# When the scans' last columns are copied out: one step later from SBUF, behind the product with C from PSUM

## The chip, the cores and the metric

The program runs on one core of one Trainium2 chip. The metric is the device time of one execution in microseconds (us). The kernel before was timed in three runs: 12873.15, 12877.57 and 12906.72 us, median 12877.57 us. One further execution was recorded by the hardware profiler; it took 12896.13 us and its span, first to last instruction, is 12894.0 us. All lines of the profile below are of that one execution.

The engines are called as in the profile: PE (TensorE, matrix products; PEld is its loading of weights), DVE (VectorE), ACT (ScalarE), POOL (GpSimd) and SP (SyncE, which here issues most of the DMA transfers). An engine works through its own instructions in the order in which they stand in its queue; an instruction that has to wait for another engine holds up all that stand behind it.

## The reference

Eight images of 64 channels and 64 x 64 pixels pass through four layers, all in float32. Layer 0 is full attention over the 4096 pixels of an image, followed by convolutions. Layer 1 is two blocks of window attention with an MLP each. Layer 2 is a dynamic 3 x 3 filter and a 1 x 9 convolution. Layer 3 is a selective scan in four directions, with norms, a gate and a convolutional mixer. The change lies in layer 3's scan:

```
def step(h, inp):                       # once per pixel, 4096 times, for each image and direction
    u_t, dt_t, B_t, C_t = inp           # u, dt: 128 channels; B, C: 16 states
    h = h * exp(dt_t[..., None] * A) + dt_t[..., None] * B_t[:, :, None, :] * u_t[..., None]
    return h, einsum('bkcn,bkn->bkc', h, C_t)
```

So each of 128 x 16 states follows its own first-order recurrence over 4096 pixels, and the output of a pixel is the sum over the 16 states of h times C.

## The kernel before

**Tiling.** The images are worked in four pairs, p = 0 to 3. An image has four directions of 4096 pixels, cut into 8 chunks of 512 (`TD`). One chunk of one direction of one image is a *unit*; a pair has 64 units. A unit's 128 channels x 16 states are taken in 8 *steps*; a step has two scans, j = 0 and j = 1, of 128 partitions x 512 pixels each (one partition is one channel with one state; two states of 64 channels lie in a tile). So a pair has 512 steps, and the whole kernel 2048 steps and 4096 scans.

**A step** (`step`, L1769 to L1807). For each j, ACT computes exp(dt * A) into a PSUM bank `dad` (L1789). DVE then scans: it takes `dad` as the factor, the tile `vd` (dt * B * u) as the addend and, unless the chunk is its row's first, the column of `carries` that was kept from the chunk before (L1792). The scan's result goes to one of two places. `own` says how many of a step's two scans DVE carries through alone: such a scan is written back into its own PSUM bank (`dad<-dad`), and DVE multiplies it with C itself (L1806 on DVE). The other scans are written to an SBUF tile `hd`, and POOL multiplies them with C, one at a time (L1806 on POOL) or both at once (L1803). `own` is 0 and 1 in turn in the first three pairs, 1 and 2 while layer 0's attention runs beside the scans (`dense`), and 1, 1, 1, 2 in the last pair.

**The copies.** The last column of each scan (the first one, where the direction runs backward) is what the next chunk's scan of the same state starts from, 8 steps later. ACT copies it into `carries`: for a scan in PSUM one column, for a scan in SBUF one column, or both columns of a step in one instruction where both scans lie in SBUF (L1794 to L1800). There are 3008 such copies. In the program they stand directly behind their scan, so j = 0's copy stands ahead of j = 1's exp, and j = 1's copy ahead of DVE's product with C. The PSUM bank is kept apart between engines: of two instructions on different engines that read one bank, the later in the program waits for the earlier. So DVE's product with C (L1806) waits for ACT's copy (L1800) of the same `dad`.

**Beside it.** POOL computes `vd` = B * (dt * u) for both scans of a step (`products`, L1767) two steps ahead. B and C of a step are two rows each, spread over 64 partitions by DMA from memory (`fetch`, L1759; SP's queue), four buffers each. PE sums the products over the states into the unit's bank `yd` (`sums`, L1818), and DVE adds it to the image's result `Y` (`gather`, L1831 to L1836). For the following unit, SP loads `xs` (`load`, L1722), PE, ACT and DVE work out dt and dt * u (`inputs` and `spread`, L1730 to L1748), and SP spreads them over the partitions into `du` (L1752), from which both the exps and POOL's products read. The exps' banks, tag `da`, are three; `inputs` takes its banks from the same three.

**The order of the work.** `scans` (L1672) goes through the 512 steps of a pair and puts pieces of other work between them: layers 0 to 2 and layer 3's preparation of the next pair (`front`) and the rest of layer 3 of the pair before (`back`), at a rate by estimated costs, so that they end 24 steps (`LEAD`) before the pair does. The first pair's front runs alone, ahead of all scans, together with layer 0 of the second. The last pair has only `back` beside it, of the pair before and then its own. This program order is not yet the engines' order: when the program is built, a scheduler places each engine's instructions by it, but lets an instruction pass others that are not yet ready by the scheduler's own estimate. In the built program many exps stand ahead of copies that precede them in the source.

Of the kernel before, what the change touches and what calls it, by code (L numbers as in the profile page):

```python
# [10 lines left out]
AF = mybir.ActivationFunctionType  # L11
# [13 lines left out]
TD = 512  # L25
NTD = L // TD
# [212 lines left out]
class _Net:  # L239
    def __init__(self, ctx, tc, x, packs, layout, out):  # L240
        self.tc, self.nc = tc, tc.nc
        self.x, self.out = x, out
        nc = self.nc
        self.const = ctx.enter_context(tc.tile_pool(name="const", bufs=1))
        self.dram = ctx.enter_context(tc.tile_pool(name="rows", bufs=2, space=bass.MemoryType.DRAM))
        self.packs, self.layout, self.w = packs, layout, {}
        self.load(self.const, (0, 1))
        with tc.tile_pool(name="temp", bufs=1) as temp:
            self.load(temp, (2,))
            self.prepare()  # L250
# [910 lines left out]
class _Direct:  # L1161
# [8 lines left out]
    def __init__(self, net, ctx):  # L1170
        self.net, self.tc, self.nc, self.w = net, net.tc, net.nc, net.w
        tc = self.tc
        self.dram = ctx.enter_context(tc.tile_pool(name="mem", bufs=2, space=bass.MemoryType.DRAM))
        self.slabs = ctx.enter_context(tc.tile_pool(name="slabs", bufs=3))
        self.ps = ctx.enter_context(tc.tile_pool(name="ps_scan", bufs=3, space=PSUM))
        self.pf = ctx.enter_context(tc.tile_pool(name="ps_front", bufs=3, space=PSUM))
        self.kept = {}
        self.turn = -1
        self.dense = 0

    def begin(self, ctx):


        tc = self.tc
        with tc.tile_pool(name="slabs0", bufs=3) as slabs, tc.tile_pool(name="w00", bufs=2) as pool:
            ahead = _Apart(self, slabs, pool).first(1)
            front = first = done = 0
            for cost in self.front(0):
                front += cost
                if cost == 0:  # L1190
                    first = front
                while first and done < AHEAD * (front - first):
                    done += next(ahead, front)
            self.run(ahead)
        one = ctx.enter_context(tc.tile_pool(name="scan1", bufs=1))
        self.Y = one.tile([P, L], F32, name="Y", tag="Y")
        self.carries = one.tile([P, NST], F32, name="carry", tag="carry")
        self.sw = ctx.enter_context(tc.tile_pool(name="scan", bufs=2))
        return front, first
# [472 lines left out]
    def scans(self, p, beside, cost):  # L1672

        self.units = []
        for im in range(2):
            out = self.memory("ys")
            self.kept["y", 2 * p + im] = out
            for nth, k in enumerate((1, 3, 0, 2)):  # L1680
                order = range(NTD) if k < 2 else range(NTD - 1, -1, -1)
                self.units += [dict(image=2 * p + im, k=k, c=c, at=at, nth=nth, out=out) for at, c in enumerate(order)]
        self.load(self.units[0])
        self.inputs(self.units[0])
        self.spread(self.units[0])
        n = 8 * len(self.units)

        late = self.back(p) if p == B // 2 - 1 else None
        steps = [{} for _ in range(n)]
        done = 0  # L1690
        for i in range(-3, n):
            if i + 3 < n:
                self.fetch(i + 3, steps[i + 3], 0)
            if 0 <= i + 2 < n:
                self.fetch(i + 2, steps[i + 2], 1)
                self.products(i + 2, steps[i + 2])
            if i >= 0:
                self.step(i, steps[i])
                for j in self.DUE[i % 8]:
                    if i + j >= 0:  # L1700
                        self.sums(i + j, steps[i + j], steps[i]["w"])
                if i % 8 == 2 and i > 8:
                    self.gather(self.units[i // 8 - 1])
                if p == B // 2 - 1 and done >= cost:
                    self.turn = max(self.turn, 0)
                while done < cost * (i + 1) / (n - LEAD):
                    done += next(beside, cost)
            if late and i >= n - 8 * (NTD - 1) and i % 8 in (3, 5, 7):
                next(late)
            if i >= 0 and i % 8 < 3 and i // 8 + 1 < len(self.units):  # L1710
                (self.load, self.inputs, self.spread)[i % 8](self.units[i // 8 + 1])
        for i in (n - 2, n - 1):
            self.sums(i, steps[i])
        self.gather(self.units[-1])
        self.run(beside)
        if late:
            self.run(late)
# [51 lines left out]
    def step(self, i, st):  # L1769

        nc, w, net = self.nc, self.w, self.net
        wk, ps = self.sw, self.ps
        u = self.units[i // 8]
        k, c, at, CC, v = u["k"], u["c"], u["at"], st["C"], st["v"]


        n0 = 2 * (i % 8)
        own = 1 + (i % 4 == 3) if u["image"] >= B - 2 else i % 2 + self.dense
        rev = k >= 2

        def along(t):
            return t[:, ::-1] if rev else t

        h = wk.tile([P, 2 - i % 2, TD], F32, name="hd", tag=f"h{i % 2}", bufs=2)
        hs = []
        for j in range(2):
            n = n0 + j
            da = self.bank("dad", (P, TD), "da")
            nc.scalar.activation(da, u["du"][:, j, 0], AF.Exp, scale=net.As[:, k, n : n + 1])  # L1789
            first = 0.0 if at == 0 else self.carries[:, n : n + 1]  # L1790
            to = da if j >= 2 - own else h[:, j]
            nc.vector.tensor_tensor_scan(along(to), along(da), along(v[:, j]), first, ALU.mult, ALU.add)  # L1792
            hs.append(to)
            if at < NTD - 1 and (own or j):  # L1794
                ends = h[:, :, 0] if rev else h[:, :, TD - 1]
                cs = self.carries[:, n0 : n0 + 2]
                if own:
                    ends = to[:, 0:1] if rev else to[:, TD - 1 : TD]
                    cs = self.carries[:, n : n + 1]
                nc.scalar.activation(cs, ends, AF.Copy)  # L1800

        if own == 0:
            st["w"] = nc.gpsimd.tensor_tensor(v, h, self.twice(CC), ALU.mult)  # L1803
        for j in range(2 if own else 0):
            engine = nc.vector if j >= 2 - own else nc.gpsimd
            m = engine.tensor_tensor(v[:, j], hs[j], CC, ALU.mult)  # L1806
            st.setdefault("w", m)  # L1807

    def sums(self, i, st, after=None):

        nc, w, net = self.nc, self.w, self.net
        wk, ps = self.sw, self.ps
        u = self.units[i // 8]
        k, c = u["k"], u["c"]
        if i % 8 == 0:
            u["y"] = ps.tile([P, TD], F32, name="yd", tag="y", bufs=1)
        for j in range(2):
            m = nc.tensor.matmul(  # L1818
                u["y"][self.HALF[j]], lhsT=w["fold"], rhs=st["v"][:, j], start=(i % 8 == 0), stop=(i % 8 == 7)
            )  # L1820
            if after is not None and j == 0:
                net.behind(m, after)
# [169 lines left out]
```

## Time and profile before

| | |
|---|---|
| median of three runs | 12877.57 us |
| profiled execution: its own time, its span | 12896.13 us, 12894.0 us |
| granted TensorE clock over the span | 0.817 of full speed |
| front of pair 0 (and layer 0 of pair 1), no scans | 0 to 2196 us |
| scans of pair 0, beside them layers 1 and 2 and layer 3's preparation of pair 1 | 2196 to 4516 us |
| scans of pair 1: beside `back` of pair 0 | 4516 to 4950 us |
| ... beside layer 0's attention of pair 2 | 4950 to 5680 us |
| ... beside the rest of pair 2's front | 5700 to 7500 us |
| scans of pair 2, in the same three parts | 7583 to 10643 us |
| scans of pair 3: with `back` of pair 2, 24 of 64 units | 10643 to about 11400 us |
| ... alone, and then with `back` of pair 3 | about 11400 to 12780 us |
| the rest of `back` of pair 3 | to 12894 us |
| ACT's copies (L1800) | 3008; 168 ns each from PSUM, 201 ns from SBUF |
| exp (L1789), scan (L1792), product with C on DVE (L1806) | 681, 1270 and 677 ns each |

A unit of 8 steps takes about 36 us in pair 0 and 33 us in pair 3. Times of waits in the profile are idle time of an engine, put down to the instruction that ended it; idle time of an engine that is not the bottleneck costs nothing by itself.

### The profile page before, as it was taken

To read this page: it belongs to the slowest core of one execution; us is meant where nothing else is said; L and a number is where in the kernel's file an instruction comes from. 1 tells how busy PE (TensorE), PEld (TensorE's weight loads), DVE (VectorE), ACT (ScalarE), POOL (GpSimd) and SP (SyncE) were. 2 spreads that over 40 slices of the span, in tenths; PEclk is the share of its full clock that TensorE was granted. 3 is DMA by queue.
4 is the path that set the end of the run, shared out by engine and by line. 5 is a ranking of instruction groups with operands and counts; after the bars stand their busy time and mean duration, and the time that the engine had idled before them with its cause. 6 is when DMAs were issued, how large, how long until landed. Compare 5 with 4: busy or idle time off the path is not lost. (4 is left out here: it accounts for less than half of the span.)

```text
span 12894.0 us, 141975 instructions
## 1 busy us (share of the span) xinstructions
PE 9714.9 (75%) x46358; PEld 3162.6 (25%) x46358; DVE 8570.4 (66%) x10061; ACT 7066.2 (55%) x15577; POOL 7760.9 (60%) x3875
## 2 busy tenths in 40 slices
PE   9999985788786558988888556997898655555556
PEld 2243421333221112224332111222342101111111
DVE  0121245788878785467776778358776778998888
ACT  5556523565646655655654645665654645455444
POOL 0000001999899883457765795347775698877774
PEclk9999976787787678988888667998888767777667
DMA  0000002555555552334443564234443456556553
GB/s 25 1 1 1 1 13 87 160 165 158 159 162 167 177 162 84 98 119 128 139 124 108 168 182 129 70 104 135 136 123 105 142 179 192 172 167 187 173 172 125
DMA packets 779985, 1579.99 MB, mean 123 GB/s; under 512 B 89312, under 2 KB 89440, under 8 KB 778208
## 3 DMA queue, kind: packets, MB, share of 16 engines
q1 hardware_dynamic: 755040, 1514.49, 38.5%
q10 hardware_dynamic: 24192, 56.32, 1.1%
q8 instruction: 367, 6.01, 0.2%
q14 instruction: 386, 3.16, 0.1%
HBM read 1199.26 MB, written 102.76 MB: 101 GB/s over the span
## 5 line engine op out<-in xcount | busy, mean ns | idle before, releaser
L1767 POOL TENSOR_TENSOR vd<-B,du 128x1024 f32<-128x1024 f32 x2048 | 4816.6, 2370 | 3728.7 <-DMA B<-rows 2391.2
L1818 PE MATMUL yd<-vd,pack 128*64 128x512 f32 x8192 | 3042.7, 782 | 1327.0 <-POOL vd L1806 648.1
L1789 ACT ACTIVATE dad<-du,As 128x512 f32<-128x512 f32 x4096 | 2734.4, 681 | 1236.0 <-DVE hd L1792 568.7
L1792 DVE TENSOR_TENSOR_SCAN hd<-dad,carry,vd 128x512 f32<-128x512 f32 x2166 | 2712.4, 1270 | 510.2 <-ACT dad L1789 295.7
L1803 POOL TENSOR_TENSOR vd<-hd,C 128x1024 f32<-128x1024 f32 x658 | 1557.8, 2367 | 648.4 <-DVE hd L1792 372.5
L1806 POOL TENSOR_TENSOR vd<-hd,C 128x512 f32<-128x512 f32 x1154 | 1484.4, 1291 | 614.9 <-DVE hd L1792 599.3
L1792 DVE TENSOR_TENSOR_SCAN dad<-dad,carry,vd 128x512 f32<-128x512 f32 x1418 | 1782.6, 1273 | 87.4 <-ACT dad L1789 87.2
L1320 ACT ACTIVATE e<-s 128x512 f32<-128x512 f32 x2048 | 1202.9, 592 | 835.4 <-PE s L1314 833.8
L1818 PEld LDWEIGHTS yd<-vd,pack 128*64 128x64 f32 x8192 | 657.3, 166 | 3329.1 <-POOL vd L1806 1120.2
L1314 PE MATMUL s<-X 64*128 64x512 f32 x4096 | 1302.2, 650 | 43.0 <-ACT e L1320 35.2
L1806 DVE TENSOR_TENSOR vd<-dad,C 128x512 f32<-128x512 f32 x1626 | 1081.4, 677 | 289.7 <-ACT carry L1800 269.0
L1306 PE MATMUL po<-e,VT 128*64 128x512 f32 x4096 | 1204.8, 625 | 7.4 <-ACT e L1320 7.2
L1800 ACT ACTIVATE carry<-hd 128x1 f32<-128x1 f32 (+1 forms) x1586 | 313.9, 201 | 741.1 <-DVE hd L1792 731.1
L1730 PE MATMUL pdd<-xs,xdt 128*128 128x512 f32 x512 | 406.0, 886 | 375.0 <-DVE hd L1792 168.7
L1472 PE MATMUL w_av<-vals,wide 64*64 64x9 f32 x16384 | 624.7, 213 | 36.4 <-ACT wide L1462 36.1
L1472 PEld LDWEIGHTS w_av<-vals,wide 64*64 64x64 f32 x16384 | 597.2, 155 | 216.7 <-issue 90.6
L1457 DVE TENSOR_TENSOR wide<-w_s,bias 128x512 f32<-128x512 f32 x512 | 329.3, 681 | 394.0 <-PE w_s L1444 389.5
L1800 ACT ACTIVATE carry<-dad 128x1 f32<-128x1 f32 x1422 | 239.0, 168 | 630.4 <-DVE dad L1792 626.3
L1314 PEld LDWEIGHTS s<-X 64*128 64x128 f32 x4096 | 355.4, 187 | 912.6 <-issue 794.3
L1329 DVE COPY att<-po 128x512 f32<-128x512 f32 x32 | 21.9, 686 | 755.9 <-PE po L1306 755.9
L1247 PE MATMUL pv<-n_sq,pack 128*128 128x512 f32 x576 | 355.8, 702 | 183.5 <-ACT n_sq L1245 175.8
L1833 DVE TENSOR_TENSOR Y<-Y,yd 128x512 f32<-128x512 f32 x128 | 125.3, 979 | 519.9 <-PE yd L1818 519.9
(246 smaller groups left out, 11236.7 us busy)
## 6 DMA issues: line engine op xcount, KB each, us to landing
B<-rows SPq DMA_DIRECT2D x2048, 256.0 KB, 3.6
C<-rows SPq DMA_DIRECT2D x2048, 256.0 KB, 3.4
du<-du SPq DMA_DIRECT2D x512, 512.0 KB, 6.1
xs<-xt SPq DMA_DIRECT2D x128, 256.0 KB, 3.7
xs<-xc SPq DMA_DIRECT2D x128, 256.0 KB, 3.8
xc<-xcv ACTq DMA_DIRECT2D x64, 256.0 KB, 2.1
zs<-z ACTq DMA_DIRECT2D x64, 256.0 KB, 3.5
xt<-XT ACTq DMA_DIRECT2D x32, 512.0 KB, 5.3
```

What stands on the lines that cost most here:

```text
L1306: nc.tensor.matmul(po[half[im]], lhsT=VT[:, t, half[im]], rhs=es[im], start=(t == 0), stop=(t == 31))
L1314: nc.tensor.matmul(ss[im], lhsT=at(half[im], t), rhs=X[half[im], jc * CH : (jc + 1) * CH], start=True, stop=True)
L1320: nc.scalar.activation(e, ss[im], AF.Exp, scale=C**-0.5, accum_out=parts[:, im, t, jc : jc + 1])
L1472: nc.tensor.matmul(self.av[half[im], x % 4 + j, h, :], lhsT=es[h // 4][half[im], j, h % 4, :], rhs=V[half[im], x + j, h, :], start=True, s ...
L1730: nc.tensor.matmul(pd, lhsT=net.xdt[:, k, :], rhs=x, start=True, stop=True)
L1767: self.nc.gpsimd.tensor_tensor(v, self.twice(st["B"]), self.units[i // 8]["du"][:, :, 1], ALU.mult)
L1789: nc.scalar.activation(da, u["du"][:, j, 0], AF.Exp, scale=net.As[:, k, n : n + 1])
L1792: nc.vector.tensor_tensor_scan(along(to), along(da), along(v[:, j]), first, ALU.mult, ALU.add)
L1800: nc.scalar.activation(cs, ends, AF.Copy)
L1803: st["w"] = nc.gpsimd.tensor_tensor(v, h, self.twice(CC), ALU.mult)
L1806: m = engine.tensor_tensor(v[:, j], hs[j], CC, ALU.mult)
L1818: m = nc.tensor.matmul(u["y"][self.HALF[j]], lhsT=w["fold"], rhs=st["v"][:, j], start=(i % 8 == 0), stop=(i % 8 == 7))
```

## The change

It touches only the copies. The copies of scans that lie in SBUF are no longer issued behind their scan, but noted in a list `ends` and issued in the next step, behind that step's exps and scans and its products with C (`carry_on`). The copies of scans that lie in PSUM are issued in their own step, but behind the products with C; so now ACT's copy waits for DVE's product, and the product waits for no copy. At the end of a pair the list is emptied (the last chunks of a row give nothing to it, so it is then empty). Number, size and engine of the copies stay as they are.

```
+        self.ends = []                      # in __init__
...
         for i in (n - 2, n - 1):
             self.sums(i, steps[i])
+        self.carry_on()
         self.gather(self.units[-1])
...
             nc.vector.tensor_tensor_scan(along(to), along(da), along(v[:, j]), first, ALU.mult, ALU.add)
             hs.append(to)
-            if at < NTD - 1 and (own or j):
-                ends = h[:, :, 0] if rev else h[:, :, TD - 1]
-                cs = self.carries[:, n0 : n0 + 2]
-                if own:
-                    ends = to[:, 0:1] if rev else to[:, TD - 1 : TD]
-                    cs = self.carries[:, n : n + 1]
-                nc.scalar.activation(cs, ends, AF.Copy)
-
         if own == 0:
             st["w"] = nc.gpsimd.tensor_tensor(v, h, self.twice(CC), ALU.mult)
         for j in range(2 if own else 0):
             engine = nc.vector if j >= 2 - own else nc.gpsimd
             m = engine.tensor_tensor(v[:, j], hs[j], CC, ALU.mult)
             st.setdefault("w", m)
+
+        self.carry_on()
+        if at < NTD - 1:
+            e = slice(0, 1) if rev else slice(TD - 1, TD)
+            cs = self.carries[:, n0 : n0 + 2]
+            if own == 0:
+                self.ends = [(cs, h[:, :, e.start])]
+            else:
+                self.ends = [(cs[:, j : j + 1], hs[j][:, e]) for j in range(2 - own)]
+                for j in range(2 - own, 2):
+                    nc.scalar.activation(cs[:, j : j + 1], hs[j][:, e], AF.Copy)
+
+    def carry_on(self):
+
+        for to, end in self.ends:
+            self.nc.scalar.activation(to, end, AF.Copy)
+        self.ends = []
```

## The prediction

> **What bounds the kernel now.** I read the busy shares first, then the busy time by stretch, then the list of waits, whole and by stretch, and last the timeline of single units.
>
> ```profile
> PE 9714.9 (75%) x46358; PEld 3162.6 (25%) x46358; DVE 8570.4 (66%) x10061; ACT 7066.2 (55%) x15577; POOL 7760.9 (60%) x3875
> ```
>
> No engine is full over the span. By stretch (each row: from:to, length, then busy us of PE, PEld, DVE, ACT, POOL; then granted clock, DMA share, GB/s):
>
> ```profile
> 2196.00:4516.00 2320.00, 1715.58 (x9120) 588.86 (x9120) 1847.67 (x2074) 1364.59 (x2672) 2095.99 (x1024) 0.78 0.54 164
> ...
> 4950.00:5680.00 730.00, 704.12 (x2461) 182.67 (x2462) 338.93 (x364) 482.42 (x1444) 284.35 (x144) 0.98 0.31 92
> 5700.00:7500.00 1800.00, 1343.47 (x8266) 514.23 (x8266) 1342.29 (x1626) 1016.20 (x1916) 1309.21 (x637) 0.79 0.44 136
> ...
> 10643.00:11800.00 1157.00, 655.50 (x1420) 146.25 (x1420) 1064.28 (x1152) 621.58 (x1356) 918.48 (x487) 0.74 0.59 179
> 11800.00:12480.00 680.00, 353.90 (x752) 79.05 (x754) 551.19 (x586) 304.74 (x733) 538.50 (x293) 0.69 0.56 174
> ```
>
> Pair 0's scans are POOL's (2096 of 2320 us, 90%). Beside the attention PE is full (704 of 730). In the middle of pair 1 (and of pair 2, 8760 to 10600, which looks the same) PE, DVE and POOL stand at 73 to 75% each: there queues wait for one another. From 10643 to 11800 it is DVE (92%). From 11800 to 12480 nobody is over 81%.
>
> The waits that the change touches (engine, line, releaser: us in total, times, longest):
>
> ```profile
> ACT carry L1800 <- DVE hd L1792: 731.1, 1030, 7.2
> ACT carry L1800 <- DVE dad L1792: 626.3, 976, 4.4
> ...
> DVE hd L1792 <- ACT dad L1789: 334.3, 178, 8.2
> ...
> DVE vd L1806 <- ACT carry L1800: 269.0, 181, 7.2
> ```
>
> ACT stands 1357 us at copies that wait for a scan; but ACT is idle 45% of the time, so that alone costs nothing. What can cost is DVE: 269 us at products that wait for a copy, and 334 us (and 92 us at scans into PSUM) at scans that wait for an exp. By stretch the 269 us are 48.8 (pair 0), 21.1 and 20.6 (the two middles), 38.1 (10643 to 11800), 117.3 (11800 to 12480), 11.8 (12480 to 12760), and 11.3 elsewhere.
>
> The 117.3 us must be read in the timeline (start, length, engine, line; in brackets the idle time before and what ended it):
>
> ```profile
> 11905.38 0.69 DVE L1806 TENSOR_TENSOR vd<-dad,C 128x512 f32<-128x512 f32 x1 [5.96 <-ACT carry L1800]
> ...
> 11928.18 3.72 POOL L1806 TENSOR_TENSOR vd<-hd,C 128x512 f32<-128x512 f32 x3
> ...
> 11930.75 1.20 SPq L1752 DMA_DIRECT2D du<-du  x2
> ...
> 11938.71 2.35 POOL L1767 TENSOR_TENSOR vd<-B,du 128x1024 f32<-128x1024 f32 x1 [6.81 <-DMA du<-du]
> ```
>
> At a unit's boundary ACT's first exp waits for the next `du`, and copies behind it hold DVE's products of the old unit. But the unit's 32.6 us are a ring without DVE: POOL starts when `du` lands (11906.05), runs without a gap to 11931.9; SP's queue waits for a C buffer that POOL's product at 11928.18 frees (to 11929.45), issues C and B, then `du` at 11930.75; that lands, and POOL goes on at 11938.71.
>
> **The change part by part.** The sum is made against the profiled execution's own 12896 us (span 12894.0), 0.14% above the median of 12877.6; a difference carries over as it is.
>
> *1. DVE's products no longer wait for a copy.* At most the 269.0 us come back, at least none. Taken: nothing of the 117.3, since POOL and SP's `du` come next and their built orders in the last pair are unchanged (8 of POOL's 4692 places differ in its last quarter, all in the first half of the pair); a third of 48.8, as POOL is the bound there, 16; half of 41.7 in the middles, 21; two thirds of 38.1 and of 11.8, DVE's own stretches, 33 (after a freed product the next scan may still want an exp that is behind the same obstacle); a third of the rest, 4. Sum -74 us.
>
> *2. Exps no longer stand behind copies of SBUF scans.* I counted in the built order of ACT, for each copy, the DVE instructions between the one it waits for and the next that needs the copy or something behind it. Before, 240 of the 1586 copies from SBUF have at most one; after, 9. What that is worth the trace does not show; above it is bounded by DVE's waits for exps where PE is not the bound (85.6 us in pair 0, 71.9 and 69.3 in the middles, 22.7 to 11800: 249.5), below by nothing. I take a tenth, 25: in pair 0 POOL is the bound, in the middles an earlier scan meets other waits. -25 us.
>
> *3. New waits: ACT's PSUM copies now wait for the product.* 1422 copies wait 0.68 us more. Behind each stand the following exps, for which DVE's scans wait, and the front's activations, for which PE waits. In the built order 83 of the 1422 have at most one DVE instruction between the product and the scan that needs what is behind; 8 have none. Such a place costs copy and exp, 0.168 + 0.681 = 0.85 us, less the 0.68 of a product or more that covers it: 8 x 0.85 + 75 x 0.17 = 20 us. Where two or more stand between (1339 places), at least 1.35 us of DVE work covers the 0.85, if ACT is not late by itself. Bounds: 0, and 83 x 0.85 = 71. +20 us. Before, 994 of the PSUM copies had at most one between, mostly the product itself: so in all the two queues are coupled at 92 tight places, where it was 1234.
>
> The Trainium skill, "PSUM — Partial Sum Buffer", section "PSUM bank collisions raise a hardware error", speaks against a gain here: two engines must never read one bank together, so one of the two readers always stands second, and the change only makes it ACT behind 0.68 us where DVE stood behind 0.17. By that rule alone the sum would be 1422 x (0.677 - 0.168) = +724 us of waiting on ACT; the trace shows 5828 us of idle ACT that can take it, and no row shows two such reads together.
>
> *4. Later copies.* A copy is wanted 8 steps on, and each `hd` tile returns 4 steps on; one step is lost of these: 0. The bank of a PSUM scan is held until the copy, 0.2 us longer than until the product; its next writer is mostly an exp, which stands behind the copy on ACT anyway; PE's `pdd`, twice a unit, can lose 0.2 us of a wait that PE's 75% hides: 0. Table loads in the built order: 888 for 891, 0.
>
> *5. The order of the rest moves.* In pairs 1 and 2 the built order has the front's work later against the steps: layer 2's products (L1588) begin at step 890, not 874; at step 932 the lag is gone. In the timeline of before, steps 744 to 872 take 705 us (5.51 each), 872 to 960 take 605 us, and 960 to 1024, with no front beside them, 267 us (4.17 each). If a step costs 4.17 and the front's work is added to that, the first part holds 171 us of front and the second 238: after, 144 steps give 771 (+67) and 72 give 538 (-67): 0. The bounds are in the rival below. SP's and POOL's orders in pairs 0 to 2 shift by a few places with it; B, C and `du` keep their distance in steps: 0.
>
> Sum: -74 - 25 + 20 = -79 us: 12,799 us against the median.
>
> **The rivals.**
>
> *A. It reaches further: about 12,580.* ACT's waits at copies hold back front work too: 254 us in pair 0, 191 and 207 in the middles. If a third of it was on a path, 217 us more come back. For it: no engine is full in the middles. Against it: POOL's 90%, and that behind a copy ACT mostly has an exp that waits for DVE again (569 and 422 us in all).
>
> *B. Swallowed: 12,840 to 12,915.* POOL is the bound in pair 0, PE beside the attention, the ring in pair 3; in the middles the next wait takes over: POOL's for PE (134 us), DVE's for PE. Then only DVE's own stretches pay, 33 us, less the 20 of part 3.
>
> *C. Slower: about 12,975.* One mechanism: steps 744 to 888 of pairs 1 and 2 keep their 5.51 us a step though less front lies beside them, because the scans' own chain (scan, product, copy, exp) sets that pace; and the later steps, where the front sets it, give nothing back. Then 16 x 5.51 = 88 us a pair, 176 in all: 12,799 + 176. For it: DVE waits there for POOL's products (55 us) and for exps (72), not for the front alone; the wait of part 3 lies in that chain. Against it: alone the scans go at 4.17. It decides from a pace of 5.17 us a step on: 144 x 5.17 is 39.5 us over today's 705 in each pair, and with the later 605 unchanged that outweighs the 79.
>
> **How the numbers follow.** This kernel can tell 0.3%, 39 us, from no change (the three runs spread by 0.26%). Chances: the forecast, a gain of 40 to 180 us, 0.46; A 0.13; B 0.14, nearly all within 0.3%; C, or another order that costs, 0.27. The forecast's own range is 12,700 to 12,840. Of A I take in the nearer part, of C down to its price: 12,640 to 12,980 leaves about 2 in 10 outside. Faster 0.59, same 0.14, slower 0.27.
>
> **What would show it.** Right: no wait of L1806 on DVE for a copy is left; a new one of ACT's copies for DVE's products takes its place, several hundred us, without longer waits of DVE's scans for exps (426 us in all before; part 2 would lower it to about 400). The unit of 32.6 us after 11800 stays, POOL still waiting for `du`. 10643 to 11800 gets shorter by some 25 us. The middles keep their length within 2%. Wrong: DVE's waits for exps grow (part 3 mis-sized); the middles get longer by 80 us each (C); the ring's period moves (then DVE or the copies were in it after all); pair 0 gets shorter by 3% or more, though POOL is 90% busy in it.

## The result, and the profile after

The changed kernel takes 12991.13 us (median of five runs, 12979.4 to 13002.3), against 12873.15 us for the kernel before, run beside it: a ratio of 1.0089 with a 95% interval of 1.0072 to 1.0106. It is 0.9% slower, some 115 us, where 79 us less were forecast; the time lies 11 us above the end of the stated range, 12,980. The profiled execution of the changed kernel has a span of 13000.3 us, 106.3 more than before, at a granted clock of 0.811 of full speed (0.817 before).

The busy shares of the changed kernel, and below them its waits that answer to those shown of before:

```profile
PE 9725.5 (75%) x46358; PEld 3176.0 (24%) x46358; DVE 8623.0 (66%) x10061; ACT 7067.0 (54%) x15574; POOL 7767.7 (60%) x3875
```

```profile
ACT dad L1791 <- DVE hd L1794: 979.4, 871, 8.3
...
ACT carry L1812 <- DVE vd L1800: 818.6, 642, 7.8
...
ACT carry L1817 <- DVE hd L1794: 375.9, 433, 3.6
DVE hd L1794 <- ACT dad L1791: 344.9, 190, 8.4
...
DVE dad L1794 <- ACT dad L1791: 150.4, 94, 4.0
```

The copies do what the diff says. The 269 us in which DVE's products waited for ACT's copies are gone: no such wait is left. In their place ACT's PSUM copies wait 818.6 us for the products. But DVE's scans now wait 495 us for exps (344.9 + 150.4; before 334.3 + 92.1 = 426), and ACT's exps wait 979.4 us for a scan (568.7 before).

Where the time went is best read against the steps, because the same step comes at another time in the two kernels. The start of a step's first exp is taken from each trace; this is how much longer (+) or shorter (-) the changed kernel takes from one such start to another, in us:

```
steps          512 of pair 0   585-684   684-872   872-888   888-928   928-1024   1024-1208   1208-1536   1536-2047
before               2320.3     769.2    1016.5     133.4     258.2      480.0      1230.4      1828.9      2128.8
after - before        +10         +18       -48       -44      +105         -4         +33         +17         +11
```

(The stretch 512 to 585, the attention, has +8.) Pair 2's middle, 1208 to 1536, repeats pair 1's: -44 in steps 1384 to 1400, +103 in 1400 to 1440. Single entries must be read with care: a kernel that keeps the order of before (the one with new copies in the old order, below) differs from before by up to 16 us in these stretches, and takes 13 us less in all, profile against profile. What stands clear of that is the +33 of steps 1024 to 1208, and the middle, where something large is given first and then taken back. The middle as a whole has little: over steps 684 to 1024, in which both kernels do the same work (8372 products of PE, 678 instructions of POOL), the changed one takes 1896.57 us against 1888.13, 8 us more, and 17 us more in pair 2's middle. The rest of the 106 us is spread over the other stretches.

What happens in the middle, the busy time by stretch shows. Each row is from:to, length, then busy us of PE, PEld, DVE, ACT, POOL, then clock, DMA share and GB/s; the rows are steps 872 to 888 and 888 to 928 of pair 1. The kernel before:

```profile
6711.84:6845.20 133.36, 114.56 (x312) 41.21 (x311) 82.39 (x102) 44.94 (x96) 58.32 (x29) 0.88 0.27 84
6845.20:7103.37 258.17, 200.62 (x498) 62.86 (x495) 178.65 (x210) 124.54 (x233) 171.77 (x85) 0.88 0.39 119
```

and the changed kernel:

```profile
6700.94:6790.39 89.45, 57.01 (x142) 14.71 (x142) 60.57 (x63) 62.88 (x113) 70.93 (x36) 0.82 0.47 143
6790.39:7153.08 362.69, 286.58 (x736) 98.80 (x734) 214.98 (x268) 135.95 (x256) 165.09 (x81) 0.87 0.28 86
```

Layer 2 begins at step 890 instead of 874, as I had counted in the built order. The 16 steps without it run at 5.6 us each, with POOL 79% busy. But then nearly all of layer 2 stands in the next 40 steps, in which PE has 736 products where it had 498, and POOL's share falls from 67% to 46%. The two rows do not hold the same share of layer 2, since before has done a part of it in the 16 steps; taken together, steps 872 to 928 take 452.1 us against 391.5, 61 more, with 68 products of PE more, and the steps 684 to 872 ahead of them 48 less, with 70 products fewer. In steps 888 to 928 of the changed kernel the waits are led by

```profile
POOL vd L1769 <- PE yd L1829: 109.1, 12, 22.3
ACT t L1594 <- PE acc L1590: 72.6, 6, 18.4
PEld acc L1590 <- DVE taps L1589: 66.7, 64, 3.6
```

In the same steps of before the first of these is 26.3 us and the third 30.4. Layer 2's products with their taps are a chain between DVE and PE, PE's sums for the scans stand in its queue behind them, and POOL, which cannot write into a `vd` before PE has read it, stops for up to 22 us at a time. In before the same stops lie mostly ahead: 46.5 us in steps 872 to 888, the longest 22.3. Nor is layer 2 much denser than it was: from its first tap to its last 285 us pass in before and 289 us in the changed kernel, over some 35 steps in both, with 74 instructions of POOL beside it against 63. Over the whole of steps 684 to 1024 POOL's wait for PE's sums grows from 134 to 167 us. So most of the 105 us is time that has moved from earlier steps; what of the rest these waits cause was not tested.

### The profile page after: what moved, and what is told of

The parts are those of the page before. It is cut to its first block, busy times and chain, and to the rows that moved or that the text cites. A ratio compares the mean times of both kernels' runs of the same rounds, so it can differ in the third digit from the quotient of the medians.

```text
span 13000.3 us, 142327 instructions
## 1 busy us (share of the span) xinstructions
PE 9725.5 (75%) x46358; PEld 3176.0 (24%) x46358; DVE 8623.0 (66%) x10061; ACT 7067.0 (54%) x15574; POOL 7767.7 (60%) x3875
## 5 line engine op out<-in xcount | busy, mean ns | idle before, releaser
L1829 PE MATMUL yd<-vd,pack 128*64 128x512 f32 x8192 | 2970.5, 777 | 1361.4 <-POOL vd L1800 737.1
L1791 ACT ACTIVATE dad<-du,As 128x512 f32<-128x512 f32 x4096 | 2761.6, 685 | 1402.3 <-DVE hd L1794 979.4
L1812 ACT ACTIVATE carry<-dad 128x1 f32<-128x1 f32 x1422 | 232.6, 164 | 820.3 <-DVE vd L1800 818.6
L1463 ACT ACTIVATE wide<-wide 128x512 f32<-128x512 f32 x512 | 309.9, 625 | 326.9 <-DVE wide L1458 196.9
```

The costliest lines, as they stand in the source:

```text
L1829: m = nc.tensor.matmul(u["y"][self.HALF[j]], lhsT=w["fold"], rhs=st["v"][:, j], start=(i % 8 == 0), stop=(i % 8 == 7))
```

## The experiments

Two theories stood against each other. **W**: the price is ScalarE's new waits for VectorE's products, in a queue in which exps and the front's activations stand behind. **O**: the price is the order of everything else, which changes because the scheduler that writes out the engines' orders places instructions by estimates in which the copies have a part. Ratios are to the kernel before, run beside each kernel.

### Halves of the change, and another LEAD

The first two kernels make one half of the change each: the SBUF copies a step later with the PSUM copies where they were, and the reverse.

```
# SBUF copies later only: in step, behind the scan
+            if at < NTD - 1 and j >= 2 - own:
+                nc.scalar.activation(self.carries[:, n : n + 1], to[:, 0:1] if rev else to[:, TD - 1 : TD], AF.Copy)
# PSUM copies behind the product only: behind the products with C
+        for j in range(2 - own, 2 if at < NTD - 1 else 0):
+            e = slice(0, 1) if rev else slice(TD - 1, TD)
+            nc.scalar.activation(self.carries[:, n0 + j : n0 + j + 1], hs[j][:, e], AF.Copy)
```

> Only the SBUF half of the change: copies of scans in SBUF one step later, copies of scans in PSUM ahead of DVE's product as before. Two theories for the 118 us that the whole change costs. W (waits): ACT stands longer at PSUM copies, behind DVE's products, and its later work is late for PE and DVE everywhere; W expects no loss here, 12,830 to 12,880. O (order): the built order has the front's work later against the steps of pairs 1 and 2, and presses it into fewer steps. Here layer 2 begins at step 882 (before 874, whole change 890) and the lag is gone at 912; O expects about a third of the loss, 12,910, all of it between steps 880 and 930.

> Only the PSUM half: copies of scans in PSUM behind DVE's product, copies of scans in SBUF directly behind the scan as before. W expects the whole loss or more, 12,980 to 13,020, since all of the new waits are here. O: layer 2 begins at step 890 as with the whole change, but its end and the norm behind it come at 910 to 920, 4 to 8 steps earlier than there; O expects about two thirds of the loss, 12,950.

The other two only change the one number LEAD: to 40 in the changed kernel, which moves the front's work earlier again, and to 8 in the kernel before, which moves it later.

> The whole change, with the program's front work spread so as to end 40 steps ahead of the pair's end instead of 24. In the built order layer 2 begins at step 878 (before 874, whole change 890) and the norm behind it at 906 (912, 920). The copies and their waits stay as in the whole change. O expects most of the loss gone, 12,880 to 12,920, the steps 888 to 936 of pair 1 shorter by some 80 us than with the whole change and the steps ahead of them longer by less. W expects the loss to stay, 12,970 to 13,010.

> The kernel before, copies untouched, with the front's work spread to end 8 steps ahead of the pair's end instead of 24. In the built order layer 2 begins at step 888 (before 874) and the norm behind it at 922 (912): nearly the lag that the change brings, without its waits. O expects about the loss of the change, 12,950 to 13,000, by steps with the same signs as there: shorter up to 888, longer after. W expects no loss, 12,860 to 12,890.

Measured: SBUF copies later alone 12998.91 us, ratio 1.0086 (1.0072 to 1.0100); PSUM copies behind the product alone 13024.5 us, 1.0108 (1.0092 to 1.0123); the changed kernel with LEAD 40 13138.43 us, 1.0197 (1.0183 to 1.0211); the kernel before with LEAD 8 12936.51 us, 1.0041 (1.0027 to 1.0056). Each half costs as much as the whole, and the first half has none of the new waits on products: that speaks against W. But O in its simple form, "the front later against the steps", failed as well: LEAD 40 brings layer 2 back to step 878 and is the slowest of all. LEAD 8 in the kernel before fell between the two ranges given for it.

### No copies, copies on VectorE, and two more LEADs

```
# no copies: lines 1794 to 1800 left out, and
-            first = 0.0 if at == 0 else self.carries[:, n : n + 1]
+            first = 0.0
# PSUM copies on VectorE, in place of line 1800
+                if j >= 2 - own:
+                    nc.vector.tensor_copy(cs, ends)
+                else:
+                    nc.scalar.activation(cs, ends, AF.Copy)
```

> All copies of the scans' last columns are left out and every scan starts at 0.0, so part of the computation is missing: the run bounds what the copies cost in all, waits included. In the order that is written out, layer 2's preparation then stands later against the steps than before, as with the whole change. Theory W (ScalarE's new waits for VectorE's products are the price): with neither copies nor waits for them the kernel is clearly faster than before, 12,600 to 12,800. Theory O (the order that follows is the price: the front's work later against the steps and pressed into fewer of them): what the copies' absence gives is lost again where layer 2 stands, so not faster than before, 12,900 or more; steps 888 to 928 longer than before by some 80 in each middle pair.

> The copies of the scans in PSUM are made by VectorE itself directly behind the scan, the SBUF ones stay on ScalarE where they were. No engine waits for a PSUM copy of another engine at all; VectorE takes some 1,500 small copies more; layer 2 stands in the order where the whole change puts it. Theory W: without the waits the kernel is as fast as before or faster, 12,860 to 12,890. Theory O: the order alone makes it slower, 12,960 to 13,010, with steps 888 to 928 longer by 60 or more in each middle pair.

> The whole change with LEAD 16 in place of 24: layer 2 begins at the same step as with the change alone, but the run of 34 instructions of layer 3's preparation without a scan (steps 912 to 928) is gone from the order. Theory O in its form 'the run without scans is the price': most of the 56 to 61 us which the change lost in steps 912 to 928 of each middle pair come back, about 12,900. Theory W: no wait is taken away, so 12,970 to 13,010.

> The kernel before with LEAD 20 in place of 24: copies as they were, the front's work moved by some six steps against the steps. Asks whether the kernel before simply sits in a favourable order whose neighbours are all slower. Theory O: some tens of us slower, 12,890 to 12,930. Theory W: the copies are untouched, so unchanged, within 40 of 12,881.

Without any copy 12867.19 us, ratio 0.9989 (0.9979 to 0.9999); PSUM copies on VectorE 12944.39 us, 1.0048 (1.0030 to 1.0067); the changed kernel with LEAD 16 13016.1 us, 1.0103 (1.0082 to 1.0124); the kernel before with LEAD 20 12990.71 us, 1.0079 (1.0056 to 1.0102). The last is the telling one: with not one copy touched, a LEAD of 20 for 24 costs nearly what the change costs. And without any copy nearly nothing is gained, in an order in which layer 2 begins at step 898. The run of layer 3's preparation without scans is not the price: LEAD 16 takes it away, and steps 912 to 928 give back 24 of 56 us, but 936 to 960 lose 35.

By number several expectations were missed: the kernel without copies and the one with copies on VectorE lie between the ranges of the two theories, and LEAD 16 and LEAD 20 above those of both. All this speaks for the order, but each of these kernels changes order and copies together. They had to be taken apart.

### Copies and order crossed

The instructions of each engine, the copies left out, are the same in both kernels and are issued by the same code in the same sequence; only the written-out order differs. So a kernel can be given the copies of one and the order of the other: behind the whole program, each instruction is tied to the one that is to stand ahead of it on its engine by a dependence that waits for nothing.

```
def in_order(tc, copies):
    traced = list(tc.nc.all_instructions())
    for engine, text in ORDER.items():
        own = [i for i in traced if ... and i.name not in copies]
        order = ...                                  # positions in the built order of the other kernel
        for a, b in zip(order, order[1:]):
            tc.add_manual_dep(own[b], own[a].name,
                mybir.DependencyInfo(mybir.DependencyClass.NoSync, mybir.DependencyReason.DATA),
                reason="order on one engine")
```

The orders of DVE (10,062 instructions), ACT (10,133 without copies), PE (23,436), POOL (3,872) and SP (5,415) then are exactly those of the other kernel. In the traces of the first two kernels below, the instructions of ACT, POOL and SP come exactly as in the kernel whose order they hold, those of DVE in all but six places and PE's products in all but 82 of 46,358. The copies fall where the scheduler puts them between: in the mean a PSUM copy stands 7.7 places behind its scan's exp on ACT (7.6 in the changed kernel, 5.7 in before).

> The copies as in the changed kernel, but every other instruction of each engine held in the order that it had in the kernel before (by dependences that fix the order on one engine and wait for nothing). Theory O (the price is the order that follows): the copies alone cost nothing, 12,780 to 12,890. Theory W (the price is ScalarE's waits for VectorE's products): the order changes nothing, 12,960 to 13,000. In between, each holds for its share.

> The reverse: the copies as before, every other instruction of each engine held in the order that it has in the changed kernel. Theory O: the order alone costs what the change cost, 12,950 to 13,000. Theory W: as before, 12,860 to 12,900. If both this and its counterpart lie well above 12,890, copies and order cost only where they do not fit each other.

> All copies left out (each scan starts at 0.0, that part of the computation is missing), every other instruction in the order of the kernel before: what the copies and all waits for them cost there, the most that any placing of them could give. My prediction's sum took 99 us of it as removable by the change. Theory W: 12,750 to 12,800. If the waits removed are only taken up by the next ones: 12,840 to 12,880.

> The kernel before with LEAD 28 in place of 24; layer 2 stays at the same step, layer 3's preparation begins some six steps earlier. How much a small shift of the order does with the copies untouched (LEAD 8 gave +54, LEAD 20 +113). Theory O: between 12,880 and 13,000. Theory W: within 40 of 12,880.

```
                     copies as before              copies as changed
order of before      12884.22                      12894.22  1.0009 (1.0001 to 1.0018)
order of after       13013.18  1.0105 (1.0089 to 1.0121)      12991.13  1.0089 (1.0072 to 1.0106)
```

No copies in the old order: 12814.07 us, 0.994 (0.9925 to 0.9956). The kernel before with LEAD 28: 12977.65 us, 1.0074 (1.0059 to 1.0088). That is settled, then: the order alone, with the copies untouched, costs the whole price (1.0105 and 1.0089 lie within each other's intervals), and the moved copies in the old order cost 0.1%. W falls. Both times lie a little beyond O's ranges, by 13 and 4 us, and far from W's. The order was not pinned with the copies of before in the order of before, but the kernels with complete computation that are pinned to it lie at 0.9999 to 1.0015, so the pinning itself costs little. Nor is the granted clock the price: it is 0.811 to 0.814 in the runs of the kernel without copies, at 12814.07 us, and 0.816 with LEAD 28, at 12977.65. The steps 888 to 928 of the kernel with old copies and new order show the same row and the same wait as the changed kernel:

```profile
6781.10:7144.68 363.58, 284.86 (x736) 97.89 (x734) 215.30 (x267) 136.12 (x257) 164.40 (x81) 0.87 0.28 86
```

```profile
POOL vd L1792 <- PE yd L1843: 110.3, 12, 22.3
```

### In which part of the new order, and what the copies cost in the old one

The two orders of an engine fall into runs that hold the same instructions and can be exchanged one by one. The largest, on DVE, ACT and PE, is the middle of a pair, where the next pair's layers 1 to 3 are prepared. One kernel takes the new order in the middles of pairs 1 and 2 alone, its counterpart everywhere else; in both the copies are those of before.

> Copies as before. The order of the changed kernel only in the middles of pairs 1 and 2 (the stretch in which the next pair's layers 1 to 3 are prepared, steps 585 to 960 and 1096 to 1450 about); elsewhere the order of before. If the price lies where layer 2 stands (theory O as I stated it first): nearly all of the +129, 12,970 to 13,010. If it is spread over the kernel: about half, 12,920 to 12,960.

> Copies as before. The order of the changed kernel everywhere but in the middles of pairs 1 and 2, where the order of before is kept: the counterpart. Price at layer 2: 12,870 to 12,900. Price spread: 12,930 to 12,980. The two together should give the +129 of the whole new order if the parts add up.

Middles alone 12950.96 us, 1.0056 (1.0038 to 1.0073); everywhere else 12952.04 us, 1.0053 (1.0035 to 1.0072). They add up to the 1.0105 of the whole, half each. In the first, steps 684 to 1024 are 40 us longer and 1208 to 1536 34 us, nothing else by more than 9; in the second the +68 of its profile are mainly +23 in pair 0, +14 in steps 585 to 684, +14 in 1024 to 1096, +19 in pair 3: no one place, and none far above the 16 us by which a stretch differed under one order.

Two further kernels hold the old order and ask what there was to gain. One has no copies, but its scans still read their column, which is zeroed once (`self.copies.add(self.nc.gpsimd.memset(self.carries, 0.0).ins.name)`, and lines 1794 to 1800 left out); the other is the kernel with the PSUM copies on VectorE.

> All copies left out (the states are not carried from chunk to chunk, that part of the computation is missing), but each scan still reads its column, which is set to zero once; every other instruction in the order of before. What copies and their waits cost in that order. If my sum was right in size: 12,780 or less. If the waits are only covered time, ended a little later by another releaser: 12,850 to 12,885, and the -70 of the kernel with constant starts was mostly the shorter scans.

> The PSUM copies made by VectorE itself, the SBUF copies on ScalarE as before, every other instruction in the order of before. In its own order this was +61. If order is the whole price there too: 12,800 to 12,885, perhaps faster than both kernels. If the copies on VectorE cost it their own time (some 1,400 by about 60 ns, 85 us): 12,900 to 12,960.

Without copies 12811.98 us, 0.9954 (0.9941 to 0.9967): some 59 us, between my two expectations. The copies do have a price, and it isn't mainly that of the scans' starts, for the kernel with constant starts (0.994) can't be told from this one by the intervals; but all of them together cost less than the 99 us that my sum took for the removable part. PSUM copies on VectorE: 12877.62 us, 0.9999 (0.9987 to 1.0010), where the same edit in its own order was 1.0048. So there too the order was the price. With it held, what goes with the product's wait and the time of the 1422 copies that VectorE makes itself cancel within the interval; a copy took 144 ns, not the 60 that I had reckoned:

```profile
L1826 DVE COPY carry<-dad 128x1 f32<-128x1 f32 x1422 | 202.4, 144 | 8.3
```

Last, each half of the change in the old order:

> Only the SBUF copies one step later, the PSUM copies as before; every other instruction in the order of before. My step 2 says -25 against before. If these copies' waits are covered by ScalarE's next waits: within 20 of before. The same edit in its own order was +117.

> Only the PSUM copies behind the product, the SBUF copies as before; every other instruction in the order of before. My steps 1 and 3 say -54 against before. If the new waits of ScalarE weigh as much as the product's waits that go: within 20 of before; if they weigh more: above 12,900. The same edit in its own order was +143.

SBUF copies later: 12900.28 us, 1.0015 (1.0006 to 1.0024), where the same edit with its own order was 1.0086. PSUM copies behind the product: 12888.22 us, 1.0004 (0.9995 to 1.0012), against 1.0108. No version was measurably faster than the kernel before and still computed everything.

### Why the removed waits brought nothing, the order held

The page of the kernel with the new copies in the old order, its scans (the last column is the idle time of DVE just before them, and what ended most of it):

```profile
L1819 DVE TENSOR_TENSOR_SCAN hd<-dad,carry,vd 128x512 f32<-128x512 f32 x2166 | 2710.9, 1269 | 571.0 <-ACT dad L1816 319.7
...
L1819 DVE TENSOR_TENSOR_SCAN dad<-dad,carry,vd 128x512 f32<-128x512 f32 x1418 | 1783.7, 1273 | 139.9 <-ACT dad L1816 123.1
```

and the same lines of before:

```profile
L1792 DVE TENSOR_TENSOR_SCAN hd<-dad,carry,vd 128x512 f32<-128x512 f32 x2166 | 2712.4, 1270 | 510.2 <-ACT dad L1789 295.7
...
L1792 DVE TENSOR_TENSOR_SCAN dad<-dad,carry,vd 128x512 f32<-128x512 f32 x1418 | 1782.6, 1273 | 87.4 <-ACT dad L1789 87.2
```

Ahead of its scans DVE is idle for 113 us more (571.0 + 139.9 against 510.2 + 87.4). Sorted by the instructions on their two sides, DVE's gaps before products fall from 290 to 52 us in the trace, 238 less; the gaps directly behind a product grow from 835 to 1019, 184 more, since the instruction behind a freed product is not ready either. DVE's waits for PE's sums (L1833 in before) go from 519.9 to 555.3. In all DVE loses 18 us of idle time, of 269 that went, and even these say little: this profiled execution is 13 us shorter than that of before, while by the medians the kernel is some 10 us longer.

That DVE comes to wait for exps instead is not the work of the copies' new place. The kernel without any copies, its columns read and the old order held, has this wait as well:

```profile
DVE hd L1818 <- ACT dad L1815: 349.5, 199, 7.0
...
DVE dad L1818 <- ACT dad L1815: 149.1, 97, 3.9
```

That is 499 us, against 426 in before, with nothing on ACT but exps and the front's work: a freed product brings the scans earlier to an exp that is not there yet.

On ACT the same is to be seen in this kernel, whose exps have nothing left to stand behind:

```profile
ACT dad L1815 <- DVE hd L1818: 1184.8, 1172, 6.6
...
ACT dad L1815 <- DVE vd L1824: 868.7, 496, 6.5
```

That is 2053 us. In before, exps waited 568.7 + 421.8 for the same two and copies 1357 beside, 2348 together. An exp needs a bank that a scan or a product of DVE gives up, so it waits for DVE whether a copy stands ahead of it or not. The copies cost what is left over, about 59 us in all of them, not 99 in the part of them that the change moves.

## Why the prediction was wrong, point by point

**What bounds the kernel.** The reading held: nobody is full over the span, POOL in pair 0, DVE from 10643 on, in the middles queues that wait for one another. That reading should have warned me about step 5: where queues wait for one another, their order can set the time.

**Step 1 with step 3 (products without a wait, -74; new waits of ACT, +20).** Together -54 were forecast; the two make up the PSUM half, which in the old order gives 1.0004, some +5 us with an interval of -6 to +15. The first term failed: I took a half to two thirds of DVE's removed waits as gains wherever I thought DVE, or no one, was the bound, with the remark that the next scan "may still want an exp that is behind the same obstacle". It did, or another wait took its place: DVE's waits for exps rose from 426 to 522 us in that kernel, and to 499 us where there were no copies at all. What step 3's term itself measures stays open, since ACT's wait for the product comes with the product's freedom; but steps 1 and 2, 99 us together, can't be right where leaving out every copy gives 59. That POOL's order in the last pair hardly moves is not so either: in the traces 84 of its 896 places there hold another instruction, all but six of them before step 1800. The ring behind that stayed, so taking nothing of the 117.3 us held.

**Step 2 (exps not behind SBUF copies, -25).** 1.0015 in the old order, +19 us. DVE's waits for exps did not fall to about 400: they are 422 us in that kernel (426 in before), so these copies held up hardly any exp for which DVE waited. In the changed kernel they rose to 495.

**Step 3's rule.** The Trainium skill's section "PSUM bank collisions raise a hardware error" of "PSUM — Partial Sum Buffer" keeps two engines from reading one bank together; by it alone I had +724 us of waiting on ACT. The trace shows 818.6 us of ACT's copies waiting for products: the size agrees. But these waits, together with those that went, changed the time in the old order by nothing that the runs can tell, so the rule says well where the wait goes and nothing of its price.

**Step 4 (later copies, banks, table loads: 0).** No run shows a cost; none was tried by itself.

**Step 5 (the order of the rest moves: 0).** This is the step that failed most: 0 forecast, 1.0105 measured, some 135 us. Its arithmetic was good for the first part. Steps 744 to 888 of pair 1 were to take 771 us and take 766.0. Steps 888 to 960 were to take 538 and take 571.8: I had let the front's work add to the steps at an unchanged price, and there it cost 34 us more. With the copies of before, the new order of the middles costs 0.56%. Half of the order's price lies outside the middles (the second hybrid, 1.0053), where I had dismissed it in half a sentence: "shift by a few places". Between the built programs 4,501 of DVE's 10,062 instructions, 9,465 of PE's 23,436 and 677 of POOL's 3,872 stand at another place.

**The sum.** -79 forecast and +115 measured: of the 194 between them some 135 lie in step 5, some 90 in steps 1 to 3 (-79 against +12), and about -30 is left over (new order 1.0105 with old copies, 1.0089 with new ones), about the most that the intervals of these ratios allow.

**The rivals.** A did not happen. B, "swallowed", is what the copies do when the order is held: 12894.22 us lies in its range. C had the right sign, and its size (12,975 against 12,991) is a coincidence. It put 88 us into the middle of each of two pairs, where the changed kernel's profile has 8 and 17 of its 106; and steps 744 to 888 did not keep 5.51 us, they fell to 5.32, while steps 888 to 928 took 105 us more in pair 1. The chance of 0.27 for "C, or another order that costs" was too low.

**What was to show it.** Right: no wait of a product for a copy; ACT's copies waiting several hundred us for products; the ring (steps 1824 to 1984, 20 units, take 653.6 us before and 654.8 after, 32.7 a unit); the middles within 2%; pair 0 not 3% shorter. Wrong: DVE's waits for exps grew; steps 1536 to 1824 are 10 us longer instead of some 25 shorter:

```profile
10738.34:11945.57 1207.23, 672.84 (x1472) 149.11 (x1472) 1108.52 (x1187) 639.81 (x1396) 951.88 (x503) 0.73 0.59 178
```

DVE is 92% busy there as before, and 14 us longer busy in the same steps (1108.5 against 1094.4).

**What stays open.** That the order is the price is shown; why this order costs is not. The part in the middles goes with POOL's longer wait for PE's sums, which was not tested by itself. Why half of the price lies in pair 0, around the attention and in pair 3, where the orders differ by a few places, was not traced to instructions. No kernel took the new order on one engine alone, so whose order it is stays open too; ACT's and SP's differ as well, in 3,654 of 10,133 and 2,087 of 5,415 places. And all orders but the one of before were slower in which the kernel was run with its computation whole, by 0.4 to 2.0%. That the order of before is a picked one among many would explain it; it is not shown.

## What to carry to other kernels

When a scheduler writes out the order, an edit has two effects, its own and the new order's, and the second can be the larger (here 1.05% against 0.1%): hold the order of all other instructions fixed (or at least change a harmless constant such as LEAD by a little) before an edit is judged by its time. A wait that is removed from one engine is a gain only if the instruction behind it has its other inputs already; ask for each what it waits for next, and let the kernel without the whole operation bound the gain from above. Where a block of other work has moved against the steps of a pipeline, compare stretches that are wide enough to hold the same work; a narrower one shows mostly time that has moved.

## What the runs showed of the hardware

A scan on VectorE that starts from a constant takes 1208 ns in the kernel without copies whose scans all start at 0.0, and one that starts from a column in SBUF 1270 ns. Over the 3584 scans that read a column this is some 220 us of DVE. It brought little, if anything: the kernel without copies takes 12811.98 us with the column read (0.9954 of before) and 12814.07 us with constant starts (0.994), though DVE's busy time is 8560.8 us in the one and 8388.0 in the other. The scans of the kernel with constant starts:

```profile
L1817 DVE TENSOR_TENSOR_SCAN hd<-dad,vd 128x512 f32<-128x512 f32 x2470 | 2944.0, 1208 | 711.2 <-ACT dad L1814 370.1
L1817 DVE TENSOR_TENSOR_SCAN dad<-dad,vd 128x512 f32<-128x512 f32 x1626 | 1946.2, 1212 | 173.7 <-ACT dad L1814 159.4
```

What DVE saved it stood idle: an upper bound from leaving work out is a bound only if one sees which engine was eased.

An instruction's duration can depend on its place in the order. VectorE's addition of the mask in the window attention, the kernel before and then the changed one:

```profile
L1461 DVE TENSOR_TENSOR wide<-wide,smask 128x256 f32<-128x256 f32 x120 | 87.0, 773 | 0.0
```

```profile
L1462 DVE TENSOR_TENSOR wide<-wide,smask 128x256 f32<-128x256 f32 x120 | 115.0, 1006 | 0.0
```

Of the 120, those that lie beside no POOL instruction take 0.415 us in both kernels (80 before, 68 after), and those that lie wholly beside POOL's work 1.68 and 1.87 us in the mean (26 and 44). It is mostly the order that moves them: 66 lie beside no POOL instruction with the old copies in the new order, 72 with the new copies in the old one. The longer additions are 28 of the 53 us by which DVE is busier in the changed kernel. The Trainium skill, "SBUF — State Buffer", section "SBUF: two separate sides", says that a VectorE instruction with two inputs in SBUF and a GpSimd one that reads SBUF take a shared port in turn, the later being blocked until the other is done. The numbers agree in kind: a product of POOL takes 1.3 to 2.4 us.
